# A Mamba scan on one Trainium2 core: gate products two tiles later, norm products a step behind their transposes, a fourth buffer for GpSimd's products

## The chip, the cores and the metric

The kernel runs on one core of one Trainium2 chip. The metric is the device time of one execution in microseconds (us). The core has five engines that work beside each other, each through its own queue in order: TensorE (PE, with PEld for its weight loads), VectorE (DVE), ScalarE (ACT), GpSimd (POOL) and SyncE (SP), which here issues most DMAs. They wait for one another through semaphores.

## The reference

The kernel computes two hybrid layers on 32 sequences of 256 tokens with 128 features: a bidirectional Mamba, a mixture-of-experts feed-forward, a recurrent block and the feed-forward again, then two attention blocks, each followed by a routed feed-forward. The change lies in the Mamba alone. It is computed twice, forward and on the flipped sequence with weights of its own, and both results are joined by a projection:

```
xn = layernorm(x, gamma, beta)            # x itself already normalised once
xc, z = split(xn @ in_w.T)                # 256 channels each
xc = silu(causal_conv(xc, 4 taps) + conv_b)
dt, B, C = split(xc @ xp_w.T)             # 8, 16 and 16 columns
delta = softplus(dt @ dtp_w.T + dtp_b)
h[t] = exp(delta[t] * A) * h[t-1] + (delta[t] * xc[t]) * B[t]     # 256 channels x 16 states
y[t] = sum over states of h[t] * C[t]  +  xc[t] * D
out  = (y * silu(z)) @ out_w.T
x = x + concat(out_forward, flip(out_backward)) @ proj_w.T + proj_b
```

## The kernel before, in words

**Tiling.** Features lie on the 128 partitions and tokens on the free axis. The 8192 tokens are 16 chunks of 512 (two sequences each). A *unit* is one chunk in one direction, so there are 32 units: 0 forward, 0 backward, 1 forward and so on. A pair of units finishes a chunk.

**A unit's chain.** It is a generator (`unit`, L409) that yields between its steps. A forward unit first normalises its chunk: centring on TensorE into a PSUM tile `m` (L421), the square `sq` and a copy `xc` on ScalarE (L423, L425), the mean of squares as four small matmuls (L432), two variants `var` on VectorE (L434, L435), their power -1/2 `rstd` on GpSimd (L437), eight transposes that spread it over the partitions (L443), and then the norm products `xin` (L449) and `xg` (L452) on VectorE, the residual on GpSimd (L450) and the convolution's input on ScalarE (L453). Both directions then do the convolution as matmuls (L463, L470), the activation (L475), `xdbl` (L481, L483, stored by L485), delta's softplus (matmul L491; ScalarE L492 to L499; `sp`, `lg`, `delta` on VectorE, L501 to L503), `du` on GpSimd (L504), the stores of delta and du (L511), the gate (matmul L514, ScalarE L523) and broadcast loads from DRAM (`bcB`, `bcC` L527; `widedelta`, `widedu` L538). The PSUM tile `m` has one buffer, which all these matmuls share.

**The scan.** 256 channels times 16 states are 32 tiles of 128 rows per unit: two halves `h` of four groups `g` of four tiles `k`. For each tile ScalarE makes `dA` (L594, three PSUM buffers), GpSimd the product `dBu` (L598, three buffers), and VectorE runs the scan (L607) over both. The states are multiplied by C: tiles k = 0 and 1 together on VectorE (L609), k = 2 on VectorE (L615), k = 3 on GpSimd (`pr`, L556, in `summed`). TensorE adds each group's four products into `yps` (L561; a first matmul L559 adds the skip term). After a half's four groups `gated` multiplies `yps` by the gate into `yg` (L576), and four matmuls (L629) and one VectorE add (L630) close a pair.

**Order.** `pipeline(unit, 16, 2 * NCH)` starts a new unit every 16 rounds and advances all active units by one yield in each round, oldest first. A scan has 16 yields, so one unit scans while the next makes its inputs and the one after that is normalised and convolved. The text's order gives priorities only: the framework's scheduler then orders each engine's instructions, and places one once its own estimate of time has the operands ready and a buffer free. An instruction may thus stand elsewhere in its engine's queue than its place in the text says. `summed` of a group is called in the next group, behind that group's first two tiles.

Of the kernel before, what the change touches and what calls it, by code (L numbers as in the profile page):

```python
# [13 lines left out]
F32 = mybir.dt.float32  # L14
# [8 lines left out]
P = 128  # L23
B, L = 32, 256
NT = B * L
CH = 512
# [248 lines left out]
def hybrid_kernel(ctx: ExitStack, tc, x_d, out_d, d, packs):  # L275
# [15 lines left out]
    def K(name):  # L291
        return cst.view(cst_t, name) if name in cst.at else cst1.view(late_t["cst1"], name)
# [10 lines left out]
    def two(ap):  # L303
        return ap.rearrange("p (b t) -> p b t", b=2)
# [48 lines left out]
    with ExitStack() as ph:  # L353
# [4 lines left out]
        def M(name):  # L358
            return mam.view(mam_t, name)

        wconv, wout, A, skip = {}, {}, {}, {}
        with tc.tile_pool(name="mtap", bufs=1) as tp, tc.tile_pool(name="mprep", bufs=2, space=PSUM) as pp:
            tap_t = tp.tile([P, tap.n], F32, name="tap_t")
            nc.scalar.dma_start(tap_t, d["tap"].partition_broadcast(P))
            for k, s in enumerate("fb"):

                wconv[s] = wp.tile([P, DCONV, DI], F32, name="wconv" + s)
                at, _, w = tap.at[s]
# [20 lines left out]
        p2 = ph.enter_context(tc.tile_pool(name="m2", bufs=2))  # L389
# [19 lines left out]
        def unit(k):  # L409
# [3 lines left out]
            def pair():  # L413
                return ps.tile([P, 2, CH], F32, tag="m", name="m", bufs=1)
# [4 lines left out]
            if s == "f":  # L419
                m = pair()  # L420
                nc.tensor.matmul(m[:, 0, :], K("center"), x, start=True, stop=True)  # L421
                sq = p2.tile([P, CH], F32, tag="ln_sq", name="sq", bufs=1)
                nc.scalar.activation(sq, m[:, 0, :], AF.Square)  # L423
                xc = p2.tile([P, CH], F32, tag="ln_xc", name="xc", bufs=1)
                nc.scalar.copy(xc, m[:, 0, :])  # L425
                yield


                m = pair()
                vps = m[:, 0, :]  # L430
                for t in range(4):
                    nc.tensor.matmul(vps[:, t : t + 1], sq[:, t * P : (t + 1) * P], K("mean"), start=True, stop=True)  # L432
                var = p2.tile([P, 8], F32, tag="ln_var", name="var")
                nc.vector.tensor_scalar_add(var[:, 0:4], vps[:, 0:4], 1e-5)  # L434
                nc.vector.tensor_scalar(var[:, 4:8], vps[:, 0:4], 1.0 + 1e-5, 1e-10, ALU.mult, ALU.add)  # L435
                rstd = p2.tile([P, 8], F32, tag="ln_rstd", name="rstd")
                nc.gpsimd.tensor_tensor(rstd, var, K("mhalf"), ALU.pow)  # L437
                yield
                yield
                m = pair()  # L440
                for n in range(2):
                    for t in range(4):
                        nc.tensor.transpose(  # L443
                            m[:, n, t * P : (t + 1) * P],
                            rstd[:, 4 * n + t : 4 * n + t + 1].to_broadcast([P, P]),
                            ident,
                        )
                xin = p2.tile([P, CH], F32, tag="xin", name="xin", bufs=1)
                nc.vector.tensor_mul(xin, xc, m[:, 0, :])  # L449
                nc.gpsimd.tensor_add(x, x, xin)  # L450
                xg = p2.tile([P, CH], F32, tag="ln_sq", name="xg", bufs=1)
                nc.vector.scalar_tensor_tensor(xg, xc, M("g"), m[:, 1, :], ALU.mult, ALU.mult)  # L452
                nc.scalar.activation(xnp[:, :, PAD : PAD + L], two(xg), AF.Identity, bias=M("b"))  # L453
                yield
            else:
                for _ in range(4):
                    yield

            m = pair()
# [65 lines left out]
            for n, at in (("B", 0), ("C", DS)):  # L525
# [1 line left out]
                nc.sync.dma_start(  # L527
                    bc[n].rearrange("p g t -> p (g t)"), rows_of(xdbl_d, at, ((0, 32), (4, 4)), 4)
                )
            for _ in range(6):  # L530
                yield


            def load(h):
                out = []
                for n in ("delta", "du"):
                    t = p2.tile([P, 4, CH], F32, tag="wide" + n, name="wide" + n)
                    nc.sync.dma_start(  # L538
                        t.rearrange("p k t -> p (k t)"), rows_of(wide_d[n], h * P, ((4, 32), (0, 4)), 4)
                    )  # L540
                    out.append(t)
                return out
# [7 lines left out]
            sums, ended = None, None  # L550
            yps = None

            def summed(h, g, prods, hs):
                nonlocal yps, ended
                pr = p2.tile([P, CH], F32, tag="prod", name="pr", bufs=4)
                nc.gpsimd.tensor_mul(pr, hs, bc["C"][:, g, :])  # L556
                if g == 0:
                    yps = ps.tile([P, CH], F32, tag="y", name="yps", bufs=1)
                    nc.tensor.matmul(yps, skip[s][:, h, :], act[:, h, :], start=True, stop=False, skip_group_check=True)  # L559
                for k, pr in enumerate([*prods, pr]):  # L560
                    nc.tensor.matmul(  # L561
                        yps[32 * k : 32 * k + 32, :],
                        K("states"),
                        pr,
                        start=False,
                        stop=(g == 3),
                        skip_group_check=True,
                        tile_position=(0, 32 * k),
                    )
                if g == 3:  # L570
                    ended = h

            def gated():
                nonlocal ended
                yg = p2.tile([P, CH], F32, tag=f"yg{s}{ended}", name="yg", bufs=1)
                nc.vector.tensor_mul(yg, yps, gate[:, ended, :])  # L576
                outs[s, ended] = yg
                ended = None

            for h in range(2):  # L580
                dw, duw = wide[h]
                for g in range(4):
                    if (h, g) == (0, 1):
                        wide.append(load(1))

                    h2 = ps.tile([P, 2, CH], F32, tag="hs", name="h2", bufs=1)
                    pr2 = p2.tile([P, 2, CH], F32, tag="prod2", name="pr2", bufs=2)
                    prods = [pr2[:, 0, :], pr2[:, 1, :]]
                    for k in range(4):
                        dA = dAs[turn[0] % 3]  # L590
                        turn[0] += 1
                        at = 16 * h + 4 * g + k
                        steps = dw[:, k, :] if s == "f" else dw[:, k, ::-1]
                        nc.scalar.activation(  # L594
                            two(dA)[:, :, 1:L], two(steps)[:, :, 1:L], AF.Exp, scale=A[s][:, at : at + 1]
                        )
                        dBu = p2.tile([P, CH], F32, tag="dBu", name="dBu", bufs=3)
                        nc.gpsimd.tensor_mul(dBu, duw[:, k, :], bc["B"][:, g, :])  # L598
                        if k == 3:
                            hs = p2.tile([P, CH], F32, tag="hs", name="hs")  # L600
                        elif k == 2:
                            h2 = ps.tile([P, 2, CH], F32, tag="hs", name="h2", bufs=1)
                            hs = h2[:, 0, :]
                        else:
                            hs = h2[:, k, :]
                        views = (hs, dA, dBu) if s == "f" else (hs[:, ::-1], dA, dBu[:, ::-1])
                        nc.vector.tensor_tensor_scan(*views, 0.0, ALU.mult, ALU.add)  # L607
                        if k == 1:
                            nc.vector.tensor_mul(pr2, h2, bc["C"][:, g, :].unsqueeze(1).to_broadcast([P, 2, CH]))  # L609
                            yield  # L610
                            if sums:
                                summed(*sums)
                        elif k == 2:
                            pr = p2.tile([P, CH], F32, tag="prod", name="pr", bufs=4)
                            nc.vector.tensor_mul(pr, hs, bc["C"][:, g, :])  # L615
                            prods.append(pr)
                    sums = (h, g, prods, hs)
                    yield
                    if ended is not None:
                        gated()  # L620
            yield
            summed(*sums)
            yield
# [2 lines left out]
            if s == "b":  # L626
# [4 lines left out]
                yield  # L631

        pipeline(unit, 16, 2 * NCH)

    late = ctx.enter_context(tc.tile_pool(name="late", bufs=1))
# [1060 lines left out]
```

## Time and profile before

| what | value |
|---|---|
| median of 3 runs | 6514.0 us (6503.61 to 6520.93) |
| the profiled execution's own time | 6514.91 us |
| its span | 6513.1 us |
| busy: PE, DVE, ACT, POOL | 5594.1, 4202.2, 2688.5, 3325.7 us |
| the Mamba's share of the span | about 2300 us, from the start |
| mean granted TensorE clock | 0.885 |

A group of instructions is given with its source line, engine, operation, output and inputs with their shapes, its count, its busy time, the mean of one in ns, and the idle time of its engine just before it with what ended it. A wait is given as engine, tile and line that waited, what it waited for, the total in us, how often, and the longest. A line of the timeline has its start, its duration, engine, line and operation, and in brackets the idle time ahead of it and what ended it. The row of a stretch has its bounds, its length, the busy time of PE, PEld, DVE, ACT and POOL with instruction counts, the granted clock, the DMA share and GB/s. The page's 40 slices show busy tenths.

### The profile page before, as it was taken

The page shows a single profiled execution, that of the slowest core. Times are in us where ns is not written, and L with a number is a line of the kernel's source. Part 1 is how long each engine was busy: PE and PEld are TensorE (multiplying, and loading weights), DVE is VectorE, ACT ScalarE, POOL GpSimd, SP SyncE. Part 2 cuts the span into 40 slices and gives each one's busy share as a digit, 9 for nine tenths or more (in the row PEclk, how much of TensorE's full clock was granted, in tenths as well). Part 3 has the DMA queues.
Part 4 walks back from the last instruction along what each step waited for, and adds up shares of the span by engine and source line. Part 5 has one row for each costly group of instructions (what it writes and reads, how often), then busy time and mean ns, then how long its engine had stood idle before and what let it go on. Part 6 is the DMA issues. An engine that isn't in the chain of part 4 may idle for free. (4 is left out here: it accounts for less than half of the span.)

```text
span 6513.1 us, 73037 instructions
## 1 busy us (share of the span) xinstructions
PE 5594.1 (86%) x25538; PEld 2738.9 (42%) x25538; DVE 4202.2 (65%) x6974; ACT 2688.5 (41%) x4391; POOL 3325.7 (51%) x3074
## 2 busy tenths in 40 slices
PE   6777777777777789999999899897998999998897
PEld 2111111111111146686544444443885444444786
DVE  5888888888888855304555555554665666664565
ACT  4555555555555435434433434433221332333221
POOL 4777777777777746304544444443332333333232
PEclk8888888888888789859999999997998999998898
DMA  3223223223223283000000000001552000000555
GB/s 149 110 92 123 104 91 118 110 95 120 104 92 119 77 331 138 1 1 1 1 1 4 9 9 8 10 9 45 188 188 67 14 17 17 17 14 11 168 186 189
DMA packets 190416, 512.20 MB, mean 79 GB/s; under 512 B 22176, under 2 KB 75168, under 8 KB 164960
## 3 DMA queue, kind: packets, MB, share of 16 engines
q1 hardware_dynamic: 172192, 468.14, 20.0%
q0 software_dynamic: 17280, 35.69, 1.6%
q8 instruction: 202, 3.31, 0.2%
q10 hardware_dynamic: 576, 3.71, 0.1%
q14 instruction: 166, 1.36, 0.1%
HBM read 360.06 MB, written 147.38 MB: 78 GB/s over the span
## 5 line engine op out<-in xcount | busy, mean ns | idle before, releaser
L598 POOL TENSOR_TENSOR dBu<-widedu,bcB 128x512 f32<-128x512 f32 x1024 | 1326.4, 1310 | 464.2 <-DVE h L607 340.3
L561 PE MATMUL yps<-pr,cst_t 128*32 128x512 f32 x2048 | 936.9, 731 | 492.2 <-DVE pr L609 214.7
L607 DVE TENSOR_TENSOR_SCAN h<-dA,dBu 128x512 f32<-128x512 f32 x768 | 941.1, 1225 | 68.9 <-POOL dBu L598 12.3
L922 POOL TENSOR_SCALAR_AFFINE_SELECT e<-e 128x2048 f32<-128x2048 f32 (+1 forms) x256 | 342.5, 1350 | 617.0 <-ACT e L1029 397.6
L561 PEld LDWEIGHTS yps<-pr,cst_t 128*32 128x32 f32 x2048 | 116.1, 117 | 1201.8 <-DVE pr L609 406.1
L594 ACT ACTIVATE dA<-widedelta,Af 128x510 f32<-128x510 f32 x512 | 348.9, 688 | 563.0 <-DVE h L607 440.4
L1392 POOL DMA_INDIRECT rows_out<-y,goes x284 | 271.8, 957 | 559.1 <-DVE y L1390 481.7
L982 DVE TENSOR_REDUCE nm<-st 128x2 f32<-128x512 f32 x512 | 324.1, 684 | 291.5 <-PE st L978 291.5
L594 ACT ACTIVATE dA<-widedelta,Ab 128x510 f32<-128x510 f32 x512 | 347.4, 687 | 394.5 <-DVE h L607 294.2
L1167 ACT ACTIVATE s<-s 128x512 f32<-128x512 f32 x284 | 178.9, 630 | 577.0 <-DVE s L1166 347.2
L315 POOL TENSOR_TENSOR rstd<-var,cst_t 128x4 f32<-128x4 f32 x128 | 130.0, 1015 | 521.5 <-DVE var L313 519.8
L767 POOL TENSOR_TENSOR comb<-comb,ye 128x512 f32<-128x512 f32 x224 | 284.8, 1275 | 181.8 <-DVE ye L766 75.2
L607 DVE TENSOR_TENSOR_SCAN hs<-dA,dBu 128x512 f32<-128x512 f32 x256 | 310.6, 1213 | 95.4 <-POOL dBu L598 95.4
L1042 ACT ACTIVATE e<-st 128x512 f32<-128x512 f32 x512 | 271.7, 598 | 175.3 <-PE st L1038 174.4
L556 POOL TENSOR_TENSOR pr<-hs,bcC 128x512 f32<-128x512 f32 x256 | 338.5, 1322 | 1.4 <-DVE hs L607 1.4
L609 DVE TENSOR_TENSOR pr<-h,bcC 128x1024 f32<-128x1024 f32 x256 | 309.8, 1210 | 8.0 <-PE yps L561 0.9
L1281 POOL DMA_INDIRECT rows_in<-xt,slot x256 | 254.0, 992 | 119.4 <-issue 99.4
L1373 PE MATMUL g_ps<-xb,gu 128*128 128x256 f32 x1136 | 302.6, 389 | 3.6 <-ACT xb L1356 2.3
L1168 DVE TENSOR_TENSOR hh<-s,u_ps 128x512 f32<-128x512 f32 x284 | 195.4, 688 | 170.2 <-ACT s L1167 164.2
L1382 PE MATMUL yps<-dn,hh 128*128 128x128 f32 x2272 | 291.0, 275 | 5.1 <-DVE hh L1168 5.1
L1373 PE MATMUL u_ps<-xb,gu 128*128 128x256 f32 x1136 | 293.3, 381 | 0.0
L1382 PEld LDWEIGHTS yps<-dn,hh 128*128 128x128 f32 x2272 | 282.6, 192 | 14.1 <-DVE hh L1168 6.6
(348 smaller groups left out, 11083.1 us busy)
## 6 DMA issues: line engine op xcount, KB each, us to landing
gu<-in_gu SPq DMA_DIRECT2D x142, 512.0 KB, 3.8
rows_in<-zero SPq DMA_DIRECT2D x60, 1170.0 KB, 18.8
widedelta<-delta_d SPq DMA_DIRECT2D x64, 1024.0 KB, 6.8
widedu<-du_d SPq DMA_DIRECT2D x64, 1024.0 KB, 5.0
dn<-in_dn SPq DMA_DIRECT2D x142, 256.0 KB, 4.0
bcB<-xdbl_d SPq DMA_DIRECT2D x32, 1024.0 KB, 7.6
bcC<-xdbl_d SPq DMA_DIRECT2D x32, 1024.0 KB, 7.3
xr<-rows_in SPq DMA_DIRECT2D x142, 130.0 KB, 3.9
```

The lines of the kernel that those rows point to most:

```text
L556: nc.gpsimd.tensor_mul(pr, hs, bc["C"][:, g, :])
L561: nc.tensor.matmul(yps[32 * k : 32 * k + 32, :], K("states"), pr, start=False, stop=(g == 3), skip_group_check=True, tile_position=(0, 32 ...
L594: nc.scalar.activation(two(dA)[:, :, 1:L], two(steps)[:, :, 1:L], AF.Exp, scale=A[s][:, at : at + 1])
L598: nc.gpsimd.tensor_mul(dBu, duw[:, k, :], bc["B"][:, g, :])
L607: nc.vector.tensor_tensor_scan(*views, 0.0, ALU.mult, ALU.add)
L609: nc.vector.tensor_mul(pr2, h2, bc["C"][:, g, :].unsqueeze(1).to_broadcast([P, 2, CH]))
L767: nc.gpsimd.tensor_add(comb, comb, ye)
L922: nc.gpsimd.affine_select(e, e, [[0, n], [sign, P]], ALU.is_gt, 0.0, base=base, channel_multiplier=-sign)
L982: nc.vector.tensor_reduce(n1[:, x, 2 * r : 2 * r + 2], o.rearrange("p (j k) -> p j k", j=2), AX.X, ALU.max, negate=True,)
L1373: nc.tensor.matmul(o[:, j, :], gu[:, at : at + P], xb, start=True, stop=True)
L1382: nc.tensor.matmul(yps[:, t, :], hh[:, k, t * P : (t + 1) * P], dn[:, k, :], start=(k == 0), stop=(k == FF // P - 1),)
L1392: i = nc.gpsimd.indirect_dma_start(rows_out[:, :], bass.IndirectOffsetOnAxis(ap=goes[:, t : t + 1], axis=0), y[:, t, :], None)
```

## The change

Three edits, with a fourth that keeps the rest of the chain in step. The gate product of a half is called behind the next half's first two tiles and their product by C (L609), just ahead of the sum that reuses `yps`, instead of ahead of these tiles; the last half's call at the unit's end stays. A yield separates the transposes from the norm products; backward units wait one yield more, so that both directions' convolutions come one step later, and the pause ahead of the first wide loads is one yield shorter, so that these and the scan keep their step. `dBu` gets a fourth buffer.

```
@@ in unit, a forward unit's norm
                             rstd[:, 4 * n + t : 4 * n + t + 1].to_broadcast([P, P]),
                             ident,
                         )
+                yield
                 xin = p2.tile([P, CH], F32, tag="xin", name="xin", bufs=1)
                 nc.vector.tensor_mul(xin, xc, m[:, 0, :])
...
             else:
-                for _ in range(4):
+                for _ in range(5):
                     yield
@@ behind the loads of bcB and bcC
-            for _ in range(6):
+            for _ in range(5):
                 yield
@@ in the scan's loops
-                        dBu = p2.tile([P, CH], F32, tag="dBu", name="dBu", bufs=3)
+                        dBu = p2.tile([P, CH], F32, tag="dBu", name="dBu", bufs=4)
                         nc.gpsimd.tensor_mul(dBu, duw[:, k, :], bc["B"][:, g, :])
...
                         if k == 1:
                             nc.vector.tensor_mul(pr2, h2, bc["C"][:, g, :].unsqueeze(1).to_broadcast([P, 2, CH]))
                             yield
+                            if ended is not None:
+                                gated()
                             if sums:
                                 summed(*sums)
...
                     sums = (h, g, prods, hs)
                     yield
-                    if ended is not None:
-                        gated()
```

More of the change, by code (lines that the diff above doesn't have):

```diff
@@ L447, in unit @@
                         )
+                yield
                 xin = p2.tile([P, CH], F32, tag="xin", name="xin", bufs=1)
@@ L455, in unit @@
             else:
-                for _ in range(4):
+                for _ in range(5):
                     yield
@@ L529, in unit @@
                 )
-            for _ in range(6):
+            for _ in range(5):
                 yield
@@ L596, in unit @@
                         )
-                        dBu = p2.tile([P, CH], F32, tag="dBu", name="dBu", bufs=3)
+                        dBu = p2.tile([P, CH], F32, tag="dBu", name="dBu", bufs=4)
                         nc.gpsimd.tensor_mul(dBu, duw[:, k, :], bc["B"][:, g, :])
@@ L610, in unit @@
                             yield
+                            if ended is not None:
+                                gated()
                             if sums:
@@ L618, in unit @@
                     yield
-                    if ended is not None:
-                        gated()
             yield
```

## The prediction

> **What bounds the kernel now.** I read the slices of the span first, then a table of busy time by stretch, then VectorE's groups and waits, then the timeline of one period.
>
> ```profile
> DVE  5888888888888855304555555554665666664565
> POOL 4777777777777746304544444443332333333232
> 300.00:2200.00 1900.00, 1437.24 (x3064) 328.49 (x3062) 1611.07 (x1513) 1030.11 (x1293) 1505.83 (x1145) 0.84 0.28 106
> ```
>
> The edits lie in the Mamba stage, slices 1 to 14 (0 to about 2300 us). In its steady part VectorE (third busy column) works 1611 of 1900 us, GpSimd 1506, TensorE 1437: VectorE sets the pace, and each microsecond in which it waits is on the path. One forward and one backward unit together take 139.5 us (L630 runs once a pair; 13 such periods lie between 138.4 and 140.3). What VectorE waits for, up to 2300 us:
>
> ```profile
> DVE yg L576 <- PE yps L561: 119.6, 63, 2.5
> DVE hs L607 <- POOL dBu L598: 95.4, 85, 2.9
> DVE xin L449 <- PE m L443: 45.3, 16, 3.9
> DVE h L607 <- POOL dBu L598: 12.3, 1, 12.3
> DVE var L434 <- PE m L432: 7.4, 3, 3.2
> ```
>
> Three waits, and the change has one part for each. The timeline shows what ends them:
>
> ```profile
> 1062.29 2.35 POOL L504 TENSOR_TENSOR du<-delta,act 128x1024 f32<-128x1024 f32 x1
> 1064.59 3.86 POOL L598 TENSOR_TENSOR dBu<-widedu,bcB 128x512 f32<-128x512 f32 x3
> 1065.88 1.22 DVE L607 TENSOR_TENSOR_SCAN hs<-dA,dBu 128x512 f32<-128x512 f32 x1 [2.15 <-POOL dBu L598]
> ...
> 1077.17 0.15 DVE L435 TENSOR_SCALAR var<-m 128x4 f32<-128x4 f32 x1
> 1077.93 1.26 POOL L556 TENSOR_TENSOR pr<-hs,bcC 128x512 f32<-128x512 f32 x1
> 1079.15 1.64 POOL L437 TENSOR_TENSOR rstd<-var,cst_t 128x8 f32<-128x8 f32 x1
> 1081.10 1.84 PE L443 MATMUL m<-cst_t,rstd 128*128 128x128 f32 x8
> 1082.98 0.69 DVE L449 TENSOR_TENSOR xin<-xc,m 128x512 f32<-128x512 f32 x1 [3.00 <-PE m L443]
> ...
> 1088.41 1.23 DVE L607 TENSOR_TENSOR_SCAN h<-dA,dBu 128x512 f32<-128x512 f32 x1
> 1088.46 1.27 POOL L556 TENSOR_TENSOR pr<-hs,bcC 128x512 f32<-128x512 f32 x1
> 1091.73 0.69 DVE L576 TENSOR_TENSOR yg<-yps,gate 128x512 f32<-128x512 f32 x1 [2.08 <-PE yps L561]
> ```
>
> First: du (2.35 us) stands in GpSimd's queue ahead of the next dBu, and with three buffers VectorE runs out. Second: xin needs the transposes, these need the power rstd, and rstd stands behind a product pr. Third: the gate needs the group's last sum on TensorE, and this needs GpSimd's pr.
>
> **The change part by part.** What counts is the order in which the scheduler puts instructions, since it places one where its own timing has it ready. I compared the built orders, counting the scans (L607) ahead on VectorE and the dBu ahead on GpSimd.
>
> *Gates.* In the built order all 64 yg stand exactly where they stood: behind the 17th scan of their half (the 16th for the very last). The text moved, the instruction did not. Is the wait in front of it shorter? pr of a group stood behind the dBu three past its group, and now stands behind the fourth past. With three buffers the dBu before pr was released by the group's fourth scan; with four, the dBu before pr is one further and is released by the same scan. So from that scan's end it is one dBu (1.24 us start to start), pr 1.26, and TensorE's pair, 1.05 to 1.92 us, before and after. Gain 0; the 119.6 us stay. The cover of this zero is GpSimd's own idle time: it waits for exactly that scan (380 us before dBu from 300 to 2200 us). Without it each pr would come one dBu later; that is the rival below.
>
> *Norm products.* xin stays where it was too (50 scans ahead of the next pair), xg too. The second var stays, rstd has the same neighbours (pr ahead, two dBu behind). So rstd, transposes and xin come as before: gain 0, 45.3 us stay. But the first var moves two scans forward (54 ahead, was 52). It needs L432, which stands on TensorE two sums earlier (behind the second group's last sum, formerly amid the third's), and xc on ScalarE, two dA earlier. Walked from the end of the fourth scan of a forward unit (k = 2 of its first group) with the durations of this trace: GpSimd dBu 1.3 to 2.2, pr 1.2, du 2.35, then three dBu and pr end at 10.7; the sum ends at 11.8, L432 (1.05) at 12.9, or 13.8 if the pair runs at 1.92. VectorE reaches var at about 12.4. A wait of 0.5 to 1.4 us, once a pair; before, var had waited once in 13. I take 0.9 x 15 pairs = 13 us lost. Bounds: 0 and 21.
>
> *The step later.* The convolution, x_dbl, delta and gate chain comes one step later in the text (a step is 139.5/32 = 4.4 us), and the closing 5 yields instead of 6 leave load() where it was. On VectorE sp, lg and delta move two scans back in backward units, at most one in forward ones; L630 moves one scan forward, its matmuls ending at 1195.4 and it starting near 1196.5, so it does not wait. ScalarE's gate comes one dA later in backward units and two earlier in forward ones; the built program keeps all 315 function loads, and dA is three tiles ahead: a load, an activation and a load back (1.28 + 1.02 + 1.28 = 3.6 us) fit into the three scans and products in hand. On SP, delta_d and du_d are stored a step later and the xdbl_d store slips behind one widedelta load in every second unit. The next reader, load(), was issued 11 to 17 us after du_d, with landings of 2.8 and 5 us, and the bc tiles are fetched some 60 us before use. Cost 0; if this cover were gone, a late load would cost its landing, 5 to 8.5 us a unit.
>
> *Fourth dBu.* This is what changes. In front of du stood three dBu not yet used, now four. In the forward unit, from the same scan: du ends at 5.8, the next dBu at 7.0; VectorE needs it at 10.3 (lg 1.5, delta 1.2, five scans, three products). In the backward unit: the dBu before du ends at 2.2, du at 4.6, three dBu at 8.3; needed at 9.4. So the 2.15 and 2.9 us waits after du go, and the four small ones (0.3 to 0.4 us, where the third buffer was just short) go too: 6.1 us a pair by position, 95.4 us in all. The single 12.3 us wait is the start of the first unit, where no buffer is ahead: it stays.
>
> *A rule against it.* du's neighbours lie beside VectorE's sp, lg and delta (L501 to L503):
>
> ```profile
> L501 DVE SCALAR_TENSOR_TENSOR sp<-sp,delta 128x1024 f32<-128x1024 f32 x27 | 46.1, 1707 | 0.0
> L502 DVE TENSOR_TENSOR lg<-lg,sp 128x1024 f32<-128x1024 f32 x28 | 38.2, 1363 | 0.0
> 1137.52 2.16 POOL L598 TENSOR_TENSOR dBu<-widedu,bcB 128x512 f32<-128x512 f32 x1 [2.36 <-DVE h L607]
> ```
>
> A dBu beside delta took 2.16 us, not 1.27, and sp had a median of 1.82 at a minimum of 1.26. The Trainium skill, "SBUF — State Buffer", section "Who interferes with whom", says that a VectorE instruction with two SBUF inputs and a GpSimd instruction that reads SBUF exclude each other, and the later one stands still for the whole of the other. By the rule a GpSimd further ahead meets these three more often as the first: six of them a pair times a full dBu of 1.27 us, less the 1.4 us paid now, is +6.2 us a pair, which would eat the gain. By the row the price already paid is 0.1 to 0.6 us an instruction, and the number of meetings need not rise, since GpSimd does no more work. I take the row: 0, with bounds of -22 and +96 us.
>
> **Sum.** -95.4 + 13 = -82 us. The profiled execution took 6514.9 us (span 6513.1 and 1.8 around it), 0.9 above the median of 6514.0. From the median: 6432 us. On all other stages TensorE and VectorE keep their orders: nothing there. A difference of 0.3% (20 us) is about what a measurement of this kernel can tell from none.
>
> **The rivals.**
>
> *Gates or norm give way too.* For it: x_dbl's successor L491 leaves the place ahead of the last group's sums in forward units, where one gate waited 2.5 us. Against it: the built positions. If half of the 165 us went as well: 6350 us.
>
> *Half of the dBu gain comes back* as longer waits at the gates, because VectorE arrives earlier at the same pr: -41 + 13, about 6486 us. For it: the gate always follows the last pr closely. Against: by my walk GpSimd has caught up (0.3 us short) at the gate behind du.
>
> *Every pr late: slower.* If GpSimd, once ahead, is no longer idle in front of the dBu that now precedes pr, every pr comes 1.24 us later; four gates and one transposition a pair wait for it: 5 x 1.24 + 0.87 (the one gate whose sum ran at 1.05 would get the 1.92) = 7.1 us x 15.5 = 110 us, against -82: 6542 us. It decides once the idle time in front of that dBu (1.0 to 1.1 us in most groups) is used up. Against: a group costs GpSimd 5 x 1.24 = 6.2 us, VectorE 7.1, so GpSimd has 0.9 us to catch up in each.
>
> *The change does nothing* is ruled out for dBu (GpSimd's order does differ), and is what I forecast of the other two parts.
>
> **How the numbers follow.** Forecast 0.62 (6400 to 6465), both more 0.12 (6350), half back 0.15 (6486, a third of it within 0.3%), late pr 0.11 (6542, partly within). Faster by over 0.3% (under 6494): 0.62 + 0.12 + 0.07 = 0.81; within 0.08; slower 0.11. The range 6390 to 6505 leaves out most of the first rival and of the last.
>
> **What would show it.** Right: hs <- dBu near 0; yg <- yps still about 120 us in 64 waits; xin <- m about 45; var <- m 10 to 25; the period of a pair 134 us instead of 139.5. Wrong: dBu waits still there behind du, or gates above 2.5 us each (pr late), or gates near 0.

## The result, and the profile after

| | before | after |
|---|---|---|
| median | 6508.8 us (6494.6 to 6520.9, 4 runs) | 6426.8 us (6423.7 to 6433.7, 4 runs) |
| ratio, with its 95% interval | 1 | 0.9881 (0.9868 to 0.9894) |
| the profiled execution's own time | 6514.9 us | 6425.4 us |
| its span | 6513.1 us | 6423.7 us |
| last L630 of the Mamba (L631 after) starts at | 2303.3 us | 2228.4 us |

The change takes 82 us off the median. The Mamba's last product starts 74.9 us earlier in the profile. The other 14.5 us between the two spans lie behind the Mamba, where the order of instructions is the same; in the nine profiles of this study that rest ranges from 4184.8 to 4209.8 us, so those 14.5 us are not put down to the change.

In the kernel after, lines from L448 on have moved down by one to three: du is L505, pr L557, the group's sum L562, yg L577, dBu L599, the scan L608. The slices of VectorE and GpSimd from the page after, and the row of the stretch from 300 to 2200 us:

```profile
DVE  5888888888888755224555555554665666665565
POOL 5888888888888655214544444443332233333332
300.00:2200.00 1900.00, 1436.81 (x3137) 334.10 (x3135) 1662.18 (x1562) 1055.57 (x1322) 1577.95 (x1186) 0.84 0.29 108
```

GpSimd's digits in the Mamba go from 7 to 8, and in the same 1900 us VectorE works 1662 us (1611 before): 51 us that it spent waiting are now work, at the same granted clock of 0.84. What VectorE waits for up to 2230 us, in the kernel after:

```profile
DVE yg L577 <- PE yps L562: 121.9, 64, 2.5
DVE xin L450 <- PE m L443: 45.2, 16, 3.9
DVE var L434 <- PE m L432: 31.5, 16, 3.1
DVE h L608 <- POOL dBu L599: 12.4, 1, 12.4
```

No scan with `hs` waits for a dBu any more: 95.4 us in 85 waits have become none. The gates (119.6 before) and the norm product (45.3) are what they were. var went from 7.4 us in 3 waits to 31.5 in 16. The end of a backward unit's du on the timeline, first before, then after:

```profile
1139.65 2.34 POOL L504 TENSOR_TENSOR du<-delta,act 128x1024 f32<-128x1024 f32 x1
1141.96 1.25 POOL L556 TENSOR_TENSOR pr<-hs,bcC 128x512 f32<-128x512 f32 x1
1143.18 5.08 POOL L598 TENSOR_TENSOR dBu<-widedu,bcB 128x512 f32<-128x512 f32 x4
1145.70 1.22 DVE L607 TENSOR_TENSOR_SCAN hs<-dA,dBu 128x512 f32<-128x512 f32 x1 [2.93 <-POOL dBu L598]
```

```profile
970.43 2.24 POOL L557 TENSOR_TENSOR pr<-hs,bcC 128x512 f32<-128x512 f32 x1
972.77 2.15 POOL L599 TENSOR_TENSOR dBu<-widedu,bcB 128x512 f32<-128x512 f32 x1
974.88 2.35 POOL L505 TENSOR_TENSOR du<-delta,act 128x1024 f32<-128x1024 f32 x1
977.19 3.73 POOL L599 TENSOR_TENSOR dBu<-widedu,bcB 128x512 f32<-128x512 f32 x3
```

(Here and below, a unit's du is the one that GpSimd makes while that unit scans; it belongs to the unit after it.) Before, du and pr stood one behind the other, and GpSimd made no dBu for 3.53 us. After, pr stands ahead of du with a dBu between them, and the pause is du alone. This is the chain's later step, not the buffer (e2 below has it with three buffers). The prediction had put that step at nothing.

**A table for all that follows.** One forward and one backward unit run L630 once. I took the 13 such periods from the second L630 to the last but one on VectorE's timeline, and summed its waits by what ended them, us per pair. "sp, lg, delta" is the busy time of L501 to L503.

| kernel | period | yg | scans <- dBu | xin | var | scans <- dA | sp, lg, delta |
|---|---|---|---|---|---|---|---|
| before | 139.45 | 7.46 | 6.13 | 2.75 | 0.09 | 0 | 8.53 |
| after | 135.17 | 7.63 | 0 | 2.78 | 1.92 | 0 | 9.00 |
| buffer alone (e1) | 135.03 | 7.63 | 1.71 | 2.58 | 0 | 0.64 | 8.54 |
| step alone (e2) | 136.60 | 7.25 | 2.07 | 2.68 | 1.31 | 0 | 8.98 |

Before to after: -6.13 for dBu, +1.83 var, +0.47 for sp, lg and delta, +0.17 gates, +0.03 xin: -3.63 of the -4.28. The last 0.65 are small gaps that I could not assign. Fifteen periods of -4.28 are -64.2 us. Another -10.7 fall before the first L630 (224.4 us before, 213.8 after). There 6.3 us of VectorE's waits are gone, 4.0 of them for dBu and 2.4 for var. Most of the other 4.4 us is no gain in itself: L630 stands earlier in VectorE's order, and one scan, one product by C, one lg and one delta that stood ahead of it now stand behind. This too comes with the step (215.0 us in e2) and not with the buffer (222.0 in e1). The two make the 74.9.

### The profile page after: what moved, and what is told of

Same layout as the page of the kernel before. It is cut to its first block, busy times and chain, and to the rows that moved or that the text cites. A ratio compares the mean times of both kernels' runs of the same rounds, so it can differ in the third digit from the quotient of the medians.

```text
span 6423.7 us, 72936 instructions
## 1 busy us (share of the span) xinstructions
PE 5521.8 (86%) x25438; PEld 2731.1 (43%) x25538; DVE 4192.9 (65%) x6974; ACT 2695.4 (42%) x4391; POOL 3357.9 (52%) x3074
## 5 line engine op out<-in xcount | busy, mean ns | idle before, releaser
L599 POOL TENSOR_TENSOR dBu<-widedu,bcB 128x512 f32<-128x512 f32 x1024 | 1323.1, 1312 | 362.9 <-DVE h L608 225.2
L562 PE MATMUL yps<-pr,cst_t 128*32 128x512 f32 x2048 | 903.5, 716 | 487.2 <-DVE pr L618 175.4
L608 DVE TENSOR_TENSOR_SCAN h<-dA,dBu 128x512 f32<-128x512 f32 x768 | 941.0, 1225 | 69.2 <-POOL dBu L599 12.4
L562 PEld LDWEIGHTS yps<-pr,cst_t 128*32 128x32 f32 x2048 | 112.0, 116 | 1171.4 <-DVE pr L618 366.4
L557 POOL TENSOR_TENSOR pr<-hs,bcC 128x512 f32<-128x512 f32 x256 | 369.3, 1443 | 2.2 <-DVE hs L608 2.2
L608 DVE TENSOR_TENSOR_SCAN hs<-dA,dBu 128x512 f32<-128x512 f32 x256 | 308.5, 1205 | 0.1
```

Source lines behind the costliest of these rows:

```text
L562: nc.tensor.matmul(yps[32 * k : 32 * k + 32, :], K("states"), pr, start=False, stop=(g == 3), skip_group_check=True, tile_position=(0, 32 ...
```

## Experiments

The theory after the result was the prediction's: the buffer gives all, the step only costs var. The rival: the step gives part itself. The first four kernels ran beside each other on one chip, the last three on another, each against its own runs of the kernel before.

Three partial versions were not run, since their built programs order every engine's instructions exactly as a kernel that was: the gates' move on top of the buffer orders them as the buffer alone; a yield between transposes and norm products with the chain kept in step orders them as before; and the chain one step later, without that split, orders them as e2. This is read from the built orders, and no run of these three shows it. If it holds, only two edits act: the fourth buffer, and the chain's later step. The traces bear out how these two divide: up to 2600 us TensorE, VectorE and ScalarE have the same order of instructions in e1 as before, and the same in e2 as after. The buffer alone moves only GpSimd's instructions against theirs.

**e1_buffer**, the fourth buffer alone:

```
-                        dBu = p2.tile([P, CH], F32, tag="dBu", name="dBu", bufs=3)
+                        dBu = p2.tile([P, CH], F32, tag="dBu", name="dBu", bufs=4)
```

> The kernel before with the fourth dBu buffer alone. Theory (the buffer carries the whole gain, the norm step costs): hs <- dBu falls from 95 us to about 0, the 12 us at the start stay, gates 120, xin 45, and var stays at 7 us because VectorE keeps the order of before: 6509 - 95 = 6414 us, about 12 us less than with all three edits (ratio 0.985). Rival (the norm step brings part of the gain, because sp, lg and delta stand later): dBu waits behind du remain in part, 30 to 50 us, time 6445 to 6465.

Measured: 6428.7 us, ratio 0.9888 (0.9871 to 0.9904): the change's whole gain within the intervals. But the waits were not as the theory had them. VectorE's waits up to 2240 us, and the timeline at a backward unit's du:

```profile
DVE yg L576 <- PE yps L561: 123.6, 64, 2.5
DVE hs L607 <- POOL dBu L598: 25.6, 15, 1.7
DVE h L607 <- ACT dA L594: 9.0, 9, 1.9
...
1108.81 2.35 POOL L504 TENSOR_TENSOR du<-delta,act 128x1024 f32<-128x1024 f32 x1
1111.12 1.27 POOL L556 TENSOR_TENSOR pr<-hs,bcC 128x512 f32<-128x512 f32 x1
1112.35 6.26 POOL L598 TENSOR_TENSOR dBu<-widedu,bcB 128x512 f32<-128x512 f32 x5
1113.64 1.22 DVE L607 TENSOR_TENSOR_SCAN hs<-dA,dBu 128x512 f32<-128x512 f32 x1 [1.71 <-POOL dBu L598]
```

pr still stands behind du, and with it a fourth tile ahead is not enough: 1.7 us stay in every backward unit, and a scan waits for dA (0.64 a pair). In return var waits for next to nothing in these periods (0.01 a pair). The theory's total came out, its mechanism did not.

**e2_norm**, the yield and the later chain, three buffers:

```
+                yield
                 xin = p2.tile([P, CH], F32, tag="xin", name="xin", bufs=1)
...
-                for _ in range(4):
+                for _ in range(5):
                     yield
...
-            for _ in range(6):
+            for _ in range(5):
```

> The kernel before with the norm step alone (yield behind the transposes, 5 instead of 4, 5 instead of 6), three dBu buffers. Theory: xin waits 45 us as before, var about 31 instead of 7, dBu waits about 95: 6509 + 24 = 6533 us (ratio 1.004). Rival (the later sp, lg and delta shorten the dBu waits behind du): dBu waits 50 to 70, time 6500 or less.

Measured: 6453.7 us, ratio 0.9929 (0.9915 to 0.9942). The theory called this slower than before; it is faster, and the rival was right. Waits up to 2260 us, and the scan behind a backward unit's du:

```profile
DVE hs L608 <- POOL dBu L599: 35.8, 56, 1.3
DVE var L434 <- PE m L432: 23.3, 16, 3.1
...
1121.50 2.35 POOL L505 TENSOR_TENSOR du<-delta,act 128x1024 f32<-128x1024 f32 x1
1123.81 3.73 POOL L599 TENSOR_TENSOR dBu<-widedu,bcB 128x512 f32<-128x512 f32 x3
1127.49 1.28 POOL L557 TENSOR_TENSOR pr<-hs,bcC 128x512 f32<-128x512 f32 x1
1128.73 3.88 POOL L599 TENSOR_TENSOR dBu<-widedu,bcB 128x512 f32<-128x512 f32 x3
1130.03 1.22 DVE L608 TENSOR_TENSOR_SCAN hs<-dA,dBu 128x512 f32<-128x512 f32 x1 [1.33 <-POOL dBu L599]
```

Three buffers, and still 60 of the 95 us of dBu waits are gone. In the backward unit pr has left the place behind du; the 1.3 us that stay are for the first dBu behind the next pr. In the forward unit pr stood ahead of du before, too. There VectorE simply asks later: the next dBu is ready 3.6 us after du starts in both kernels, and the scan that needs it could start at 1.45 us before and starts at 3.92 in e2. By place, us each:

| place of the wait for a dBu | before | e1 (buffer) | e2 (step) | after |
|---|---|---|---|---|
| behind du, forward unit | 2.1 | 0 | 0 | 0 |
| behind du, backward unit | 2.9 | 1.7 | 1.3 | 0 |
| the small ones | 0.4, 0.4, 0.3 | 0 | 0.4, 0.4 | 0 |

So buffer and step take away the same waits: by the periods -4.42 alone, -2.85 alone, -4.28 together. On top of the buffer, the step takes the last 1.71 of dBu and 0.64 of dA, and pays 1.92 for var and 0.47 for sp, lg and delta.

**e3_gates**, the gates' call moved, nothing else:

```
                             yield
+                            if ended is not None:
+                                gated()
                             if sums:
                                 summed(*sums)
...
-                    if ended is not None:
-                        gated()
```

> The kernel before with the gates' call moved alone. The built order is that of before on all five engines. Theory: nothing, 6509 us (ratio 0.999 to 1.001), gates 120 us. Rival (the text's place changes the waits that the framework writes into the program): gates' wait shorter by some 10 us or more.

Measured: 6503.4 us, ratio 1.0 (0.9991 to 1.0008), with the order of before on every engine (the trace has it so for TensorE, VectorE, ScalarE and GpSimd up to 2600 us). The gates' wait up to 2300 us is the 119.6 us of before:

```profile
DVE yg L576 <- PE yps L561: 121.1, 64, 2.4
```

**e4_pinned**, the buffer and the gates' move, but made to happen: an ordering edge that holds no semaphore ties each yg behind the last paired product by C (L609) that is written ahead of it.

```
+        def behind(ins, mark):
+            tc.add_manual_dep(
+                ins.ins,
+                mark.ins.name,
+                mybir.DependencyInfo(mybir.DependencyClass.NoSync, mybir.DependencyReason.DATA),
+                reason="behind",
+            )
...
-                nc.vector.tensor_mul(yg, yps, gate[:, ended, :])
+                behind(nc.vector.tensor_mul(yg, yps, gate[:, ended, :]), marks[-1])
...
-                            nc.vector.tensor_mul(pr2, h2, bc["C"][:, g, :].unsqueeze(1).to_broadcast([P, 2, CH]))
+                            mark = nc.vector.tensor_mul(pr2, h2, bc["C"][:, g, :].unsqueeze(1).to_broadcast([P, 2, CH]))
+                            marks.append(mark)
```

> Fourth buffer, gates' call moved, and each gate product tied by an ordering edge behind the last paired product by C that the text has ahead of it, so that it does stand later in VectorE's queue: three scans and a paired product later in the middle of a unit, six scans and more at its end. Theory (the wait is a matter of place, VectorE is the bound): the 122 us at the gates fall to below 15, nothing takes their place but some microseconds at var: 6414 - 105 = about 6305 us. Rival (GpSimd becomes the bound, or the sums that reuse yps start late and hold the paired products): dBu or product waits of 50 us or more appear, 6360 to 6400 us.

Measured: 6337.9 us, ratio 0.9752 (0.9739 to 0.9765). One gate on the timeline, and the waits up to 2140 us:

```profile
1054.73 0.67 DVE L586 TENSOR_TENSOR yg<-yps,gate 128x512 f32<-128x512 f32 x1
...
DVE var L444 <- PE m L442: 66.7, 16, 4.2
DVE xin L459 <- PE m L453: 39.6, 16, 3.9
DVE hs L617 <- POOL dBu L608: 27.3, 16, 1.7
```

The gates' waits are gone: what the text's move alone did not do, an edge does, and it is worth another 91 us beside e1. The expectation of 6305 us missed var: an earlier VectorE reaches it before its sum, 4.24 us a pair.

**e5_var_back** is the kernel after with its first var tied behind the product of the third group's third tile (k = 2), so that it no longer waits:

```
-                nc.vector.tensor_scalar_add(var[:, 0:4], vps[:, 0:4], 1e-5)
+                shifted = nc.vector.tensor_scalar_add(var[:, 0:4], vps[:, 0:4], 1e-5)
+                if len(closes) > 3:
+                    behind(shifted, closes[-3])
...
-                            nc.vector.tensor_mul(pr, hs, bc["C"][:, g, :])
+                            closes.append(nc.vector.tensor_mul(pr, hs, bc["C"][:, g, :]))
```

> The changed kernel with the first var tied by an ordering edge behind the third group's product by C (k = 2), so that it stands about as late as in the kernel before. Theory (var moved ahead of its means L432, and VectorE waits there 1.9 us a pair): var falls from 31 to below 8 us, xin, gates and dBu stay at 45, 122 and 0: period 135.2 - 1.7 = 133.5 us, 25 us less in all (ratio to before about 0.984). Rival (what is waited for, the power on GpSimd, only moves the wait on): xin grows by as much and the time is that of the changed kernel, ratio 0.988.

Measured: 6368.9 us, ratio 0.9788 (0.9775 to 0.9802). The period is 131.59 us, 3.58 less than after, of which var's wait is 1.92. The waits up to 2240 us, and the place of xin on the timeline:

```profile
DVE yg L589 <- PE yps L574: 119.7, 64, 2.5
DVE xin L462 <- PE m L455: 22.5, 16, 3.9
...
1023.21 0.15 DVE L447 TENSOR_SCALAR var<-m 128x4 f32<-128x4 f32 x1
1024.88 1.65 POOL L449 TENSOR_TENSOR rstd<-var,cst_t 128x8 f32<-128x8 f32 x1
1028.59 0.69 DVE L462 TENSOR_TENSOR xin<-xc,m 128x512 f32<-128x512 f32 x1 [1.71 <-PE m L455]
```

xin's wait fell by half, which I had not forecast; this is the other 1.6 us of the 3.58. Moving var moved rstd on GpSimd: a dBu now stands between it and the pr that it followed, it starts 1.67 us behind the second var, where after has 2.72 (910.62 to 913.34), and xin stands one scan later.

**e6_after_pinned** is the kernel after with the gates tied as in e4; **e7_after_pinned_xin** also ties xin behind the product of the fourth group's third tile:

```
-                nc.vector.tensor_mul(xin, xc, m[:, 0, :])
+                norm = nc.vector.tensor_mul(xin, xc, m[:, 0, :])
+                if len(closes) > 3:
+                    behind(norm, closes[-3])
```

> The changed kernel (all three edits) with each gate product tied behind the last paired product that the text has ahead of it, as in e4. Theory (the buffer needs the later chain to clear the waits behind du): gates 0, dBu 0 instead of the 27 us that stayed in e4, and var, which the built order puts two scans later than in e4, below 15 us instead of 67: period about 125 us, 6338 - 70 = 6270 us (ratio 0.964). Rival (GpSimd, busy 112 us of each pair, is the bound by now): dBu waits come back at 2 us a pair or more, 6300 us or above.

> As e6, and xin tied behind the fourth group's product by C (k = 2), two scans, a paired and a single product later. Theory: the 2.4 us a pair at xin go as well: period about 122.5 us, 6235 us (ratio 0.959). Rival (what follows xin comes later, so the convolution and the next unit's activation, or GpSimd's x, hold something else): other waits of 2 us a pair take its place and the time is that of e6.

Measured: e6 6305.2 us, ratio 0.9690 (0.9677 to 0.9703), a period of 128.06; e7 6286.1 us, ratio 0.9651 (0.9638 to 0.9665), a period of 126.22. Both fell short of their forecasts of 6270 and 6235 us. In e6 the dBu waits did not come back (0.14 us a pair), so its rival is not the cause; but xin waits 3.35 us a pair (2.78 after), and scans wait 1.10 for dA. The waits of e7 up to 2085 us and its row of the stretch from 300 to 2050 us show what holds it:

```profile
DVE sp L514 <- ACT lg L512: 37.4, 16, 28.9
DVE h L620 <- ACT dA L607: 25.9, 30, 2.0
DVE hs L620 <- ACT dA L607: 16.2, 15, 1.1
DVE var L444 <- PE m L442: 7.3, 12, 3.1
...
300.00:2050.00 1750.00, 1255.61 (x3088) 310.58 (x3086) 1630.75 (x1539) 1034.01 (x1308) 1525.46 (x1167) 0.83 0.31 116
```

Neither gate nor xin waits (of sp's 37.4 us, 28.9 are the start of the first unit, as in every kernel here); ScalarE's dA is late now (42 us), and VectorE works 93% of the stretch (1631 of 1750 us), with GpSimd at 87%. e7 is the fastest of all, ahead of both kernels: its gate and norm products really do stand later, by an order that the scheduler cannot undo.

## Why the prediction was right, and where it was not

The size held: -82 us forecast, -82 by the medians. The steps held unevenly.

- *Gates: 0.* Right, and shown: 119.6 us before, 121.9 after, and e3 gives 1.0. The reason, that GpSimd's idle time covers the later pr, held at three gates of a pair. At the fourth, behind a backward unit's du, that idle time is used up: GpSimd sat idle for 1.2 us in the last 9 us ahead of this gate before and for none after, and the wait went from 1.56 to 1.83 us in each of 13 periods. The rival of the late pr rests on just this; it came true at one gate in four, for 0.27 us.
- *Norm products: 0.* Right for the yield and for xin (45.3 to 45.2 us).
- *Fourth dBu: 95.4 us gone, the 12.3 stay.* Right as to what goes (0 and 12.4 us), wrong as to what does it. "Needed at 9.4" in the backward unit, against a dBu ready at 8.3, was walked in the order of the changed kernel, where pr already stands ahead of du. I took that order to be the buffer's work. With the buffer alone pr stays behind du, and 1.7 us of the 2.9 stay. I also wrote of four small waits a pair; there are three.
- *The step later: cost 0.* This is the step that failed. It gains 2.85 us a pair alone, since it puts pr ahead of du in backward units and lets VectorE ask later in forward ones; it costs var and 0.47 us of VectorE's own work; and on top of the buffer it comes to about nothing (-4.42 without it, -4.28 with it).
- *First var: 0.9 us a pair, 13 in all, at most 21.* Mis-sized: 31.5 us against 7.4, so +24. Two lengths of the wait are seen. The timeline after has both, and below it stand the rows of the two stretches:

```profile
905.10 1.05 PE L562 MATMUL yps<-pr,cst_t 128*32 128x512 f32 x2 [0.51 <-POOL pr L557]
906.08 1.05 PE L432 MATMUL m<-cst_t,sq 128*128 128x1 f32 x8
907.17 0.16 DVE L434 TENSOR_SCALAR var<-m 128x4 f32<-128x4 f32 x1 [0.95 <-PE m L432]
...
1172.66 1.92 PE L562 MATMUL yps<-pr,cst_t 128*32 128x512 f32 x2 [0.51 <-POOL pr L557]
1174.50 1.87 PE L432 MATMUL m<-cst_t,sq 128*128 128x1 f32 x8
1176.41 0.16 DVE L434 TENSOR_SCALAR var<-m 128x4 f32<-128x4 f32 x1 [2.63 <-PE m L432]
...
905.10:907.13 2.03, 2.03 (x10) 1.10 (x10) 1.12 (x1) 1.17 (x2) 2.03 (x2) 1.00 0.00 0
1172.66:1176.37 3.71, 3.71 (x10) 1.96 (x10) 1.11 (x1) 1.16 (x2) 3.62 (x3) 0.50 0.00 0
```

  The granted clock (third from the end of a row) tells them apart: 1.00 in the first stretch, 0.50 in the second. It does so in all 13 periods: five waits of 0.93 to 0.95 us with L432 at a clock of 1.00, eight of 2.41 to 2.63 us with it at 0.50. My walk had 0.5 us with a fast pair of sums and 1.4 with a slow one. About 0.4 us was missing in both, and in the slow case 0.8 more: I let the pair run at 1.92 us but kept L432 at 1.05. The two follow each other and are slow together, and 1.92 + 1.87 is 1.7 us more than 1.05 + 1.05. That the 0.9 I took is close to the waits at full clock is chance.
- *The rule against it: took the row, 0, between -22 and +96.* The number was near: sp, lg and delta cost 0.47 us a pair more (9.00 against 8.53), about 7 us in 15 pairs, and e1 (8.54) and e2 (8.98) show that it comes with the step. But to set the row against the rule was wrong, for the trace follows the rule. These are VectorE's lg and delta, and GpSimd's products beside them, in the kernel after:

```profile
966.99 3.48 POOL L599 TENSOR_TENSOR dBu<-widedu,bcB 128x512 f32<-128x512 f32 x2 [0.78 <-DVE hs L608]
969.87 1.68 DVE L503 TENSOR_TENSOR lg<-lg,sp 128x1024 f32<-128x1024 f32 x1
970.43 2.24 POOL L557 TENSOR_TENSOR pr<-hs,bcC 128x512 f32<-128x512 f32 x1
972.60 1.20 DVE L504 TENSOR_TENSOR delta<-lg,du 128x1024 f32<-128x1024 f32 x1
972.77 2.15 POOL L599 TENSOR_TENSOR dBu<-widedu,bcB 128x512 f32<-128x512 f32 x1
```

  Each time the later of two pays for what is left of the earlier. lg starts while a dBu has 0.60 us to go, and takes 0.47 longer than its 1.21; pr starts while lg has 1.12 us to go, and takes 0.98 longer than its 1.26; dBu starts while delta has 1.03 us to go, and takes 0.88 longer, and delta, the earlier, keeps its 1.20. What the prediction mis-sized is the rule's sum: six whole products a pair, all paid by VectorE. Six meetings a pair did come, but with GpSimd as the later: six of its dBu and pr in each pair take over 2.1 us, where before about four did, and GpSimd does not set the pace. VectorE is the later in four, by 0.1 to 0.6 us each, 1.7 us a pair in all against 1.2 before.
- *The sum.* Per pair it was -6.1 + 0.9 = -5.2 and came out -4.28; the 134 us forecast for a period were 135.2. The start of the stage made up for much of that (-10.7 us ahead of the first L630), and the 14.5 us behind the Mamba are in no step. The match to the microsecond is partly luck. Two smaller sums were off: half of the dBu gain is 48 us and not 41, which puts that rival at 6479 us; and the chances count a half of it as within 0.3%, not the third that is named.
- *The rivals.* Every pr late came at one gate in four and no further. Half back did not come at the gates (+0.17 us a pair); what was given back was at var. "Gates give way too" needed the edge of e4.

## What to carry to other kernels

When two edits of one change touch the same queue, do not walk the final order and credit it to one of them: build each alone and see which neighbours change, for the gains may be the same waits counted twice. A text's order is a wish where a scheduler places instructions; a wait at a product whose input is late goes only when the product really moves behind other ready work, and an ordering edge does that (a ratio of 0.9752 where the buffer alone gives 0.9888). Each removed wait brings the next one nearer (dBu, then var, then dA), so forecast the remainder after the next-latest operand, not the sum of waits. And where a chain of matmuls ends a wait, bound it with all its links at the slow clock together.

## What the runs showed of the hardware

- TensorE's granted clock switches between full and half inside a stage whose mean is 0.84 before and after, and small groups of matmuls on the path take the one or the other: L432's eight records 1.05 or 1.87 us, a pair of sums 1.05 or 1.92, the eight transposes L443 1.09 or 1.97. A kernel can meet the same one every time: in e4 L432 runs at 0.50 in all 13 periods, and each wait for it is 4.24 to 4.25 us. What makes the clock switch at a given moment is left open here.
- A VectorE instruction that reads two tiles from SBUF (sp, lg, delta) and a GpSimd product stand in each other's way, and the later one pays. From 300 to 2200 us in the kernel after, a dBu that starts behind delta overlaps it by 1.04 us and takes 0.89 longer, 13 times out of 13, while delta takes its usual 1.20; an lg that starts behind a dBu overlaps it by 0.60 us and takes 0.47 longer. VectorE's products by C, whose states lie in PSUM, keep their length beside GpSimd's (1.19 to 1.23 us for 128x1024).
